# Second mixing after the dense step, norm's turning a step on, closer steps at the end: one schedule edit in a two-layer macaron network

## The chip, the cores and the metric

The kernel runs on one core of a Trainium2 chip. The metric is the device time of one execution in microseconds, the median of several runs. The profile is one execution, recorded by the hardware profiler. The engines are PE (TensorE), DVE (VectorE), ACT (ScalarE), POOL (GpSimd) and SP (SyncE, which issues DMAs).

## The reference, cut to what matters

2048 tokens (4 x 512) of width 128 pass through two macaron layers. Layer 0 is a routed expert network, a linear attention and the expert network again. Layer 1 is a product-key expert network, an attention of 16 heads whose scores are refined by a small network over all heads, and the product-key network again. The change lies in the last two of these, which the kernel computes joined.

```python
# attention of layer 1: the scores of all heads are mixed twice
attn_t = jnp.transpose(scores, (0, 2, 3, 1))
combined = jnp.concatenate([attn_t, kerple_t], axis=-1)
hdn = jax.nn.gelu(jnp.dot(combined, w1) + b1, approximate=False)
refined = jnp.dot(hdn, w2) + b2
scores = scores + kerple[None] + jnp.transpose(refined, (0, 3, 1, 2))
weights = jax.nn.softmax(jnp.where(causal, scores, -jnp.inf), axis=-1)
out = jnp.einsum('bhij,bhjd->bhid', weights, v)
# feed-forward of layer 1 behind it
q = (x @ Wq).reshape(b, t, 2, H, RET // 2)
sim = jnp.einsum('btphn,hkpn->pbthk', q, keys)
# top 8 of x keys, of y keys, of their 64 sums -> idx, scores
w = jax.nn.silu(jnp.einsum('btd,bthkd->bthk', x, down_embed[idx])) * jax.nn.softmax(scores)
x = x + 0.5 * (einsum('bthk,bthkd->btd', w, up_embed[idx]) + swiglu(x, Wg, bg, Wu, bu, Wd, bd))
```

## The kernel before, in words

`attn` (from line 976) holds the last two sublayers. It runs over 16 token tiles of 128 queries, four a batch. A tile with index `ib` in its batch sees `(ib + 1) * 128` keys. A **unit** (line 1176 on) is the part of a tile whose softmax is taken at once: the whole tile for `ib` 0 and 1, half a tile for 2 and 3. A unit is made of **pairs**: two for `ib` 0, four otherwise; 88 pairs in all. Names such as 11.1.6 say tile 11, half 1, row group 6.

A loop over **steps**, counted by `k` (lines 1341 to 1423), writes the order by hand. The four engines PE, DVE, ACT and POOL run strictly in that order (`manual_schedule`); one loop turn is a step, and nothing waits at its end: each engine goes on to the next step as soon as its own data are there. A step has, in this order:

- loads of the pair two steps on (SP; the pairs' score tiles F have ten buffers),
- `mix2` (line 1102) of the pair that was first mixed two steps before: 16 matmuls (L1107), then 2 to 8 reductions on DVE (L1118). If that pair was *busy*, its `mix2` comes only after the next two items,
- what is due by `at`: a unit's `norms` (L1194, L1196), `values` (L1217, L1229), `project` (L1234, L324), an expert tile's `norm` (L297) and `best` (L77, L78); then the turning of one pair of a finished unit (L1158, copied by L1164); then `middle`: the expert product (`turn`, `weigh`, `finish`: L184, L187, L199, L204) or the `gate` (L1289),
- either the **dense step** of an expert tile (L1272 on PE, then L1281 and L1283 on ACT), or `mix1` of the next pair: 32 matmuls (L1083) into a PSUM tile named `four`,
- `exps` of an expert tile if due (L118, L144, L153 with 4 exponentials), then the pair's GELU (L1098). A pair that comes right behind a unit's exponentials is *busy*: DVE copies it out of PSUM (L1094) and the GELU reads the copy,
- what is due by `end`: `near` (L84), `far` (L96), `tops` (L108, L111), `replace` (L118), `select` (L159), `heads` (L164, L166, L168), `last` (L174, L177), `turned` (L303, copied by L305), `add` (L324), and `finished`, which takes a tile's statistics (DVE L287, L288, then POOL L290, L291),
- if the step completed a unit, its exponentials (L1133: 16 for `ib` 0 and 1, 8 for the others), and, if an expert tile is ready, `norm8` (L133, L140) ahead of them. A step with both is called a **burst** here. `keys` of the next expert tile (L1262, L1264) come here too.

Two memories decide much. `four` takes half of PSUM and has one buffer, so `mix1` and the dense step follow one another through it: the next one starts when the GELU, the copy (L1094) or the gate has read the last one out. All small PSUM tiles are named `one` and go round four buffers: `mix2` takes two, a turning one or two, all others one.

A burst at step `k` sets the dense step to `k + 3`, the selection to `k + 4`, the expert product to `k + 7`. If a unit's softmax falls on the step ahead of the dense step, the dense step is put off by one. Written out, the loop takes 129 steps (0 to 128); the last `mix1` stands in step 100. Bursts stand in steps 19, 23, 31, 40, 44, 50, 57, 66, 70, 76, 83, 92, 96 and 102, dense steps among the mixings in 22, 26, 34, 43, 47, 54, 60, 69, 73, 80, 86, 95 and 99. ACT loads its function table anew whenever it goes from exponentials to GELU or to SiLU (dense) and back.

Of the kernel before, what the change touches and what calls it, by code (L numbers as in the profile page):

```python
# [211 lines left out]
class Net:  # L212
# [771 lines left out]
    def attn(self, out):  # L984

        nc, tc = self.nc, self.tc
        with (
# [11 lines left out]
            class Pair:  # L999
# [53 lines left out]
                def load(u):  # L1053

                    J, m = u.J, 2 * u.n
                    u.F = sf.tile([P, m, SEQ // u.n], FP, tag="F", name="F")
                    for half in range(2):
                        x = u.t.S[u.q0 + 4 * half : u.q0 + 4 * half + 4]
                        nc.sync.dma_start(
                            u.F[half::2, :, :J],  # L1060
                            bass.AP(
                                x.tensor, x.offset, [[SEQ, 4 * H], [-GQ * H * SEQ, m], [1, J]]
                            ),
                        )
# [239 lines left out]
            todo, middle, weights, late, stored = {}, {}, {}, {}, []  # L1304

            def at(k, f, *a):
                todo.setdefault(k, []).append((f, a))
# [4 lines left out]

            waiting, mixed, turns = list(pairs), {}, []
            ready, routed, last_u = [], None, None
            dense, turned, busy, k = -1, 0, False, 0

            def load(n):
                if n < len(pairs):
# [3 lines left out]
            def values_of(t):  # L1322
                v = s1.tile([P, H * DH], FP, tag="v", name="v", bufs=6)
                nc.sync.dma_start(v, t.v)
                vs[t.n] = v

            def finished(t):

                u = Experts(t.n)
                at(k + 1, u.norm)  # L1330
                end(k + 1, u.turned)
                end(k + 4, ready.append, u)

            def end(k, f, *a):
                late.setdefault(k, []).append((f, a))

            def run(todo):
                for f, a in todo.pop(k, ()):
                    f(*a)
# [4 lines left out]
            while len(stored) < NT:  # L1344
                if waiting and dense != k:
                    load(len(pairs) - len(waiting) + 2)
                second = mixed.pop(k - 2, None)
                if second and second is second.unit.parts[0] and not second.unit.q0:
                    values_of(second.t)
                if second and not second.busy:  # L1350
                    second.mix2()
                run(todo)
                if turns and turns[0][1] <= k:
                    p = turns.pop(0)[0]
                    p.turn()
                    if p is p.unit.parts[-1]:
                        n = max(k + 1, p.unit.end + 5)
                        at(n, p.unit.values)
                        if p.unit.q0 + p.unit.nq == P:
                            at(n + 1, project, p.t)  # L1360
                            end(n + 1, finished, p.t)
                run(middle)
                if second and second.busy:
                    second.mix2()
                first = None
                if dense == k:
                    last_u.dense()
                    middle.setdefault(k + 1, []).insert(0, (last_u.gate, ()))
                elif waiting:
                    first = waiting.pop(0)  # L1370
                    first.mix1(busy)
                    mixed[k], busy = first, False
                run(weights)
                if first:
                    first.gelu()
                    if waiting:
                        waiting[0].masks()
                run(late)

                full = second.unit if second and second is second.unit.parts[-1] else None  # L1380
                experts = fresh = None
                if routed and k >= routed.soonest and (full or not waiting and not mixed):
                    experts, routed = routed, None
                busy = busy or full is not None or experts is not None
                if not routed and ready:
                    routed = fresh = ready.pop(0)
                    fresh.soonest = k + 4
                    fresh.keys()
                if experts:
                    nc.scalar.preload_act_table_set("natural_log_exp_and_others")  # L1390
                    experts.norm8()
                if full:
                    full.softmax()
                    full.end = k + int(experts is not None)
                    late.setdefault(full.end + 2, []).insert(0, (full.invert, ()))
                    at(full.end + 3, full.norms)
                    if dense == k + 1 and waiting:
                        dense = k + 2
                    turns.extend((p, k + 2) for p in full.parts)
                if experts:  # L1400
                    u = last_u = experts
                    dense, turned = (k + 3 if waiting else max(k + 1, turned)), k + 7
                    weights[k + 1] = [(u.replace, (2, 3)), (u.shift, ()), (u.exps, ())]
                    end(k + 4, u.select)
                    end(k + 4, u.heads)
                    end(k + 6, u.last)
                    middle.setdefault(k + 7, []).extend(
                        (g, ()) for g in (u.turn, u.weigh, u.finish)
                    )
                    end(k + 7, u.add)  # L1410
                    at(k + 11, u.store)
                if fresh:
                    u = fresh
                    end(k + 1, u.near)
                    at(k + 2, u.best)
                    end(k + 2, u.far)
                    end(k + 3, u.tops, 0, 1, 2, 3)
                    end(k + 4, u.replace, 0, 1)
                k += 1
# [107 lines left out]
```

## Time and profile before

| what | value |
|---|---|
| median of 3 runs | 1616.69 us (1616.16 to 1617.67) |
| the profiled execution | 1613.29 us |
| its span, first to last instruction | 1611.5 us |
| PE busy | 1235.9 us (77%) |
| DVE busy | 933.4 us (58%) |
| ACT busy | 836.9 us (52%) |
| POOL busy | 828.2 us (51%) |
| first `mix1` (step 0) | 899.1 us |
| `mix1` of step 31, 57, 83, 96 | 1063.8, 1239.6, 1411.5, 1494.5 us |
| last `mix1` (step 100) | 1523.0 us |

How to read it: the times of the steps are the starts of the 32 matmuls of L1083 in that step, read off the timeline of PE, which runs them in the order of the loop. A row of the timeline has the start in us from the span's start, the time taken, engine, line, operation, what it writes and reads, the count of merged instructions, and in brackets the engine's idle time before it with what ended it. A row of the waits has the waiting engine and its tile, what it waited for, the sum in us, the number of waits and the longest.

### The profile page before, as it was taken

How to read it: one execution, taken by the hardware profiler on the slowest of the kernel's cores; microseconds unless marked ns; L12 is line 12 of the kernel's file. 1: busy time of each engine (PE TensorE's matmuls, PEld its weight loads, DVE VectorE, ACT ScalarE, POOL GpSimd, SP SyncE). 2: the span in 40 equal slices, each digit the busy share in tenths (PEclk: the TensorE clock that was granted, in tenths of full speed). 3: DMA queues.
4: the chain of work that ended last, by engine and by line, in shares of the span. 5: the costliest groups of instructions: out<-in, count | busy, mean ns of one | idle time of the engine just before them, and what ended most of it. 6: DMA issues, size and time to landing. Idle time of an engine off the chain costs nothing.

```text
span 1611.5 us, 32621 instructions
## 1 busy us (share of the span) xinstructions
PE 1235.9 (77%) x12520; PEld 800.2 (50%) x12520; DVE 933.4 (58%) x2540; ACT 836.9 (52%) x1653; POOL 828.2 (51%) x835
## 2 busy tenths in 40 slices
PE   5769989965888479888887588777778778777763
PEld 2446756643554255555663144554446445454462
DVE  6443422234543988787852267766757666766853
ACT  4211232211222657676654678855866666776752
POOL 4444232235443898888867046346544455436423
PEclk8889799977989689999998899889898889888986
DMA  4662032304220013444457977665555445545100
GB/s 101 153 165 54 0 68 59 73 15 106 53 54 0 0 53 137 159 145 166 156 199 261 289 212 208 200 178 155 138 162 180 129 148 149 168 127 151 30 11 4
DMA packets 182822, 194.08 MB, mean 120 GB/s; under 512 B 44058, under 2 KB 155018, under 8 KB 182538
## 3 DMA queue, kind: packets, MB, share of 16 engines
q1 hardware_dynamic: 181242, 190.87, 41.2%
q8 instruction: 99, 1.62, 0.4%
q10 hardware_dynamic: 1296, 1.11, 0.3%
q14 instruction: 57, 0.47, 0.1%
q0 software_dynamic: 128, 0.01, 0.0%
HBM read 139.96 MB, written 52.13 MB: 119 GB/s over the span
## 4 chain that ended last, share of the span: by engine, by line
PE 42%; DVE 17%; ACT 16%; POOL 14%; issue 7%; DMA 3%; SPq 1%; POOLq 0%; ACTq 0%; DVEq 0%
PE po L436 4%; ACT F L1133 4%; ACT ht L1098 4%; PE ph L1083 3%; PE pq L924 3%; PE pd L1272 3%; PE po L1217 3%; PE pf L1107 3%; POOL al L84 2%; PE pu L425 2%; ACT al L153 2%; PE pk L527 2%; PE pt L1158 2%; PE pg L423 2%; PE pu L549 2%
## 5 line engine op out<-in xcount | busy, mean ns | idle before, releaser
L1071 POOL TENSOR_TENSOR F<-F,kz 128x512 f32<-128x512 f32 (+10 forms) x88 | 164.3, 1869 | 78.3 <-ACT F L1133 61.1
L1118 DVE CUSTOM_DVE_ANT_0 F<-pf,F 128x64 f32<-128x64 f32 (+21 forms) x256 | 99.0, 435 | 143.4 <-PE pf L1107 121.6
L84 POOL TENSOR_TENSOR al<-sim 128x512 f32<-128x512 f32 x128 | 129.3, 1041 | 60.0 <-ACT sim L1264 51.5
L1098 ACT ACTIVATE ht<-ph,b 128x2048 f32<-128x2048 f32 (+7 forms) x65 | 102.1, 1571 | 107.8 <-PE ph L1083 107.7
L427 ACT ACTIVATE g<-pg 128x512 f32<-128x512 f32 x72 | 42.5, 597 | 184.8 <-PE pg L423 122.9
L1083 PE MATMUL ph<-rows,w1s 32*32 32x512 f32 (+16 forms) x2816 | 97.2, 580 | 50.8 <-issue 27.3
L1107 PE MATMUL pf<-ht,w2b 64*32 64x512 f32 (+16 forms) x1408 | 94.2, 561 | 47.3 <-ACT ht L1098 44.6
L1133 ACT ACTIVATE F<-F,mn 128x64 f32<-128x64 f32 (+21 forms) x256 | 129.5, 507 | 0.1
L164 POOL TENSOR_TENSOR al<-al 128x1152 f32<-128x1152 f32 x16 | 42.0, 2626 | 163.2 <-DVE al L159 130.7
L938 ACT ACTIVATE st<-pq 128x256 f32<-128x256 f32 (+3 forms) x128 | 82.8, 699 | 68.7 <-issue 37.9
L1158 PE MATMUL pt<-ident,F 128*128 128x128 f32 x640 | 102.8, 305 | 17.4 <-DVE mn L1118 7.6
L432 POOL TENSOR_TENSOR hT<-g,spread 128x512 f32<-128x512 f32 x64 | 79.6, 1266 | 65.3 <-DVE g L431 41.6
L1164 DVE COPY wT<-pt 128x512 f32<-128x512 f32 (+1 forms) x176 | 104.3, 632 | 11.9 <-PE pt L1158 10.0
L924 PE MATMUL pq<-k,q 32*128 32x256 f32 (+3 forms) x1024 | 101.7, 487 | 11.1 <-POOL q L901 8.2
L1158 PEld LDWEIGHTS pt<-ident,F 128*128 128x128 f32 x640 | 81.2, 157 | 50.1 <-ACT F L1133 18.8
L1217 PEld LDWEIGHTS po<-wT,v 128*64 128x64 f32 x2560 | 85.0, 150 | 24.6 <-issue 14.3
L118 DVE MATCH_REPLACE8 rep<-top,al 128x576 f32<-128x576 f32 x128 | 94.4, 741 | 0.0
L1217 PE MATMUL po<-wT,v 128*64 128x64 f32 x2560 | 88.6, 235 | 6.2 <-DVE wT L1164 4.8
L425 PE MATMUL pu<-ln_xT,w 128*128 128x512 f32 x144 | 80.3, 641 | 8.2 <-DVE g L431 4.8
L436 PEld LDWEIGHTS po<-w,hT 128*128 128x128 f32 x576 | 75.5, 213 | 8.4 <-POOL hT L432 5.4
L436 PE MATMUL po<-w,hT 128*128 128x128 f32 x576 | 77.2, 298 | 2.8 <-POOL hT L432 2.8
L894 DVE TENSOR_TENSOR t<-p,cos 128x512 f32<-128x512 f32 x64 | 43.8, 685 | 58.4 <-POOL k L902 34.2
(217 smaller groups left out, 2957.7 us busy)
## 6 DMA issues: line engine op xcount, KB each, us to landing
spread<-rows SPq DMA_DIRECT2D x24, 1024.0 KB
S<-st SPq DMA_DIRECT2D x32, 512.0 KB
S<-st SPq DMA_DIRECT2D x32, 384.0 KB
V<-v SPq DMA_DIRECT2D x16, 512.0 KB
S<-st SPq DMA_DIRECT2D x32, 256.0 KB
v<-V SPq DMA_DIRECT2D x16, 512.0 KB
rows<-near SPq DMA_DIRECT2D x12, 524.0 KB
F<-S SPq DMA_DIRECT2D x24, 256.0 KB
```

The costliest lines, as they stand in the source:

```text
L84: nc.gpsimd.tensor_tensor(u.al[:, h, :NEAR].rearrange("p (i j) -> p i j", j=NK), bc(u.sim[:, 0, h, :TK], 2, NK), bc(u.sim[:, 1, h], 1, TK) ...
L425: nc.tensor.matmul(pu, self.w3[:, c * P : (c + 1) * P], xT, start=True, stop=True)
L436: nc.tensor.matmul(po, hT[:, c, i * P : (i + 1) * P], self.w2[:, c, :], start=(c == 0), stop=(c == NCH),)
L924: nc.tensor.matmul(pq[hh // 2][:, hh % 2, :J], u.q[r, t, a, :], u.k[r, t, a, :J], start=(a == 0), stop=(a == 1), tile_position=(hh * 32, 0),)
L1071: nc.gpsimd.tensor_tensor(u.F[:, :, :J], u.F[:, :, :J], win, ALU.add)
L1083: nc.tensor.matmul(ph[32 * x : 32 * (x + 1), r, :, :J], self.w1s[at], u.G[x ^ 1][at], start=True, stop=True, tile_position=(32 * r, 32 * x),)
L1098: nc.scalar.activation(u.ht[:, :, :, : u.J], u.x, AF.Gelu, bias=self.b1)
L1107: nc.tensor.matmul(pf[c][32 * r : 32 * (r + 1), :, :J], self.w2b[at].rearrange("p h a -> p (h a)"), u.ht[at, r, :, :J], start=True, stop=True,
L1133: nc.scalar.activation(F, F, AF.Exp, bias=mn[:, g : g + 1], scale=-1.0, accum_out=sm[:, g : g + 1],)
L1158: nc.tensor.transpose(pt[:, at : at + P], u.F[:, m - 1 - s0 - s, j * P : (j + 1) * P], self.ident,)
L1164: nc.vector.tensor_copy(u.unit.wT[:, js.start : js.stop, :, q : q + w * GQ].rearrange("p j h (r q) -> p j h r q", q=2), pt[:, : len(js) * ...
L1217: nc.tensor.matmul(po[o * DH : (o + 1) * DH, c, :], vs[u.t.n - u.t.ib + j][:, h * DH : (h + 1) * DH], u.wT[:, j, h, x : x + nq], start=(j ...
```

## The change

Only the loop's bookkeeping changes; no instruction is added, dropped or resized.

- `mixed` now holds the step in which a pair's second mixing is due. It is two steps on as before, but three for the pairs first mixed in the two steps behind a burst, and never before the pair ahead of it. With the dense step at `k + 3`, those two second mixings come in the steps `k + 4` and `k + 5`, where before they came in `k + 3` and `k + 4`.
- `turned` comes two steps behind a tile's statistics, not one, while pairs are left. The tile is ready for its keys three steps behind, not four (one, once no pair is left).
- A tile may not start its burst until five steps behind its keys, not four, while pairs are left.
- The rule that put off a dense step behind a softmax is dropped.
- Once no pair is left, selection and heads come a step earlier behind the burst, last, product and add two steps earlier, and the next dense step may come two steps earlier.

```diff
-                end(k + 1, u.turned)
-                end(k + 4, ready.append, u)
+                end(k + 2 if waiting else k + 1, u.turned)
+                end(k + 3 if waiting else k + 1, ready.append, u)
...
-                second = mixed.pop(k - 2, None)
+                second = mixed.pop(k, None)
...
-                    mixed[k], busy = first, False
+
+                    due = max(due + 1, k + (3 if k in (burst + 1, burst + 2) else 2))
+                    mixed[due], busy = first, False
...
-                    fresh.soonest = k + 4
+                    fresh.soonest = k + (5 if waiting else 4)
...
-                    if dense == k + 1 and waiting:
-                        dense = k + 2
...
-                    u = last_u = experts
-                    dense, turned = (k + 3 if waiting else max(k + 1, turned)), k + 7
+                    u, burst = experts, k
+                    last_u = u
+                    dense, turned = (k + 3 if waiting else max(k + 1, turned)), k + (7 if waiting else 5)
...
-                    end(k + 4, u.select)
-                    end(k + 4, u.heads)
-                    end(k + 6, u.last)
-                    middle.setdefault(k + 7, []).extend(
+                    n = 0 if waiting else 1
+                    end(k + 4 - n, u.select)
+                    end(k + 4 - n, u.heads)
+                    end(k + 6 - 2 * n, u.last)
+                    middle.setdefault(k + 7 - 2 * n, []).extend(
...
-                    end(k + 7, u.add)
+                    end(k + 7 - 2 * n, u.add)
```

Written out, the loop now takes 126 steps, with the last `mix1` in step 99. Bursts stand in steps 19, 24, 31, 40, 45, 50, 57, 66, 71, 76, 83, 92, 97 and 102, dense steps among the mixings in 22, 27, 34, 43, 48, 53, 60, 69, 74, 79, 86 and 95, and dense step 12 in 100. Around the burst of step 57 (pairs 10.0.0 to 10.0.6), PE has:

| step | before | after |
|---|---|---|
| 58 | mix2, values 8, mix1 (busy), turned 7 | mix2, values 8, mix1 (busy) |
| 59 | mix2, project 8, turning, mix1 | mix2, project 8, turning, mix1, turned 7 |
| 60 | turning, mix2 (busy pair of 58), dense 6, turned 8 | turning, dense 6, keys 7 |
| 61 | mix2 (of 59), norms 9, turning, mix1, keys 7 | norms 9, turning, mix2 (busy pair of 58), mix1, turned 8 |
| 62 | turning, mix1 (busy) | mix2 (of 59), turning, mix1 |

On DVE the gate of step 61 stood behind the reductions of that step's mix2; now it stands ahead of them. From the end of the mixings on, PE's order was: dense 12, the last mix1, mix2, values 15.0, product 12, dense 13, keys 14, turnings, values 15.1, project 15, product 13, dense 14, turned 15, keys 15, product 14, dense 15, product 15. It is now: the last mix1, dense 12, mix2, mix2, turning, keys 14, values 15.0, turning, product 12, dense 13, turnings, product 13, dense 14, values 15.1, project 15, turned 15, keys 15, product 14, dense 15, product 15. On POOL, heads 14 stand ahead of the statistics of tile 15, where they stood behind them.

More of the change, by code (lines that the diff above doesn't have):

```diff
@@ L1314, in attn @@
             ready, routed, last_u = [], None, None
-            dense, turned, busy, k = -1, 0, False, 0
+            dense, turned, burst, due, busy, k = -1, 0, -9, 0, False, 0
             def load(n):
```

## The prediction

> **What bounds the kernel now.** I read the waits of the joined part first. It runs from 890 us to the end, and all of the change lies in it.
>
> ```profile
> engine line waited for: us in total, times, longest us
> PE pf L1107 <- ACT ht L1098: 44.6, 15, 6.2
> PE ph L1083 <- issue: 27.3, 13, 2.7
> PE pw L184 <- POOL ws L166: 23.0, 2, 16.5
> PE lt_pt L303 <- DVE lt_xn L297: 16.3, 8, 3.2
> ```
>
> These waits of TensorE are what the change touches: second mixings (L1107) behind a GELU, first mixings (L1083) after a dense step, the expert tail, norm's turning (L303). Are they on the path? I took dense step 60 in the timeline, ScalarE first, then TensorE, then VectorE.
>
> ```profile
> 1255.84 1.31 ACT L1098 ACTIVATE ht<-ht,b 128x1216 f32<-128x1216 f32 x1
> ...
> 1257.20 1.33 ACT L1098 ACTIVATE ht<-ph,b 128x1280 f32<-128x1280 f32 x1
> ```
> ```profile
> 1257.20 1.27 PE L1107 MATMUL pf<-ht,w2b 64*32 64x304 f32 x16 [6.20 <-ACT ht L1098]
> 1258.59 2.04 PE L1272 MATMUL pd<-lt_xT,downT 128*128 128x128 f32 x8
> 1260.45 1.06 PE L1272 MATMUL pd<-lt_xT,wg 128*128 128x128 f32 x8
> ...
> 1266.98 1.29 PE L1083 MATMUL ph<-rows,w1s 32*32 32x336 f32 x32 [2.02 <-issue]
> ```
> ```profile
> 1265.76 1.12 DVE L1289 SCALAR_TENSOR_TENSOR hT<-pd,bu,hT 128x128 f32<-128x128 f32 x4
> ```
>
> The two GELUs queue behind ScalarE's exponentials. The dense products (L1272) start 0.06 us after the second GELU ends (1258.53): they write the one PSUM tile that this GELU reads. In 11 of the 13 dense steps among the mixings this distance is 0.05 us. So the 6.2 us belong to ScalarE, and the second mixing in front of the dense step hides inside them. The 2.02 us put to "issue" end when the gate (L1289) lets that tile go, at 1266.88. From dense end to first mixing the 13 dense steps take 66.2 us, 4.4 to 6.7 each.
>
> **The change, part by part.**
>
> *Second mixings moved past the dense step.* Nothing is saved ahead of it: it still waits for the second GELU. Behind it, VectorE today does the second mixing's reduction (0.9 to 1.3 us), sT 0.27, wT 1.29, gate 1.12, so 5.1 us with the matmuls at dense step 73. After, the gate stands ahead of the reduction: pn 0.27, half the turning 0.5, wT 1.3, gate 1.1 make 3.2 to 3.4 us, with the moved mixing (1.1) beside it. Gain: 1.9 (step 22), 1.1 (34, a key matmul of 1.0 between), 1.1 (43), 1.7 (47), 0.3 (60, key matmul), 1.4 (69), 1.7 (73), 0.3 (86), 1.4 (95): 10.9 us offered.
>
> *A price that the waits view doesn't show.* Dense step 60's first eight matmuls took 2.04 us, the next eight 1.06. The Trainium skill ("TensorE: Matmul & The Clock Gate", Part 1) says that the array runs at half clock after an idle window, until about 3.4 us of activity. The row agrees: slow from 1257.20 to about 1260.5. Today the second mixing spends 1.3 us of that; after, the dense step spends all and takes about 4.9 us (step 86 took 4.88). From the rows 4.11, 4.59, 3.82, 4.15, 4.88, 4.77 that adds 0.8+0.3+1.1+0.7+0+0.1 = 3.0 us. By the plain count of matmuls it would be nothing. I take half, 1.5, as some of it falls where VectorE is last anyway.
>
> *Norm's turning one step on.* Of 16.3 us, those at steps 33 (3.2), 58 and 84 (1.3 each) lie in front of the same ScalarE wait: nothing. Those at 31 (1.3 of 2.2), 39, 65, 91 (2.8, 2.3, 2.3) and 15 (1.0) stand on the chain: 9.7 us offered. But the norm itself stays on VectorE in its step:
>
> ```profile
> 1288.59 2.15 DVE L297 TENSOR_SCALAR lt_xn<-x,lt_mv,lt_rs 128x128 f32<-128x128 f32 x1
> 1290.46 1.01 DVE L1164 COPY wT<-pt 128x512 f32<-128x512 f32 x2
> ```
>
> Behind it queue wT and the reduction, which free the four small PSUM tiles ("one") that the next second mixing needs. I worked step 60 to 66 through. Keys come a step earlier, so tops (0.9) and replace (1.5) now precede the statistics; norm runs 1288.9 to 1291.0, wT to 1292.0, reduction to 1293.0; turning and first mixing of step 66 start at 1293.0 and 1293.9 (before 1294.12); the exponentials at 1300.4 (before 1300.38). Gain nil. The norm took 0.33 us elsewhere and 2.15 with a mask running on GpSimd. The skill ("SBUF — State Buffer", Who interferes with whom) says that tensor_scalar can contend with GpSimd for a shared port pair, and the loser waits for a whole instruction. With 0.33 all of this would be 1.8 us sooner, 5.5 over three places; I keep the row's 2.15.
>
> *The rule that put the dense step off after a softmax is gone.* At 26, 54 and 80 the dense step now comes right behind 16 exponentials (5.75 us) and two table loads (1.28 each). I worked steps 66 to 83: first mixing at 70 is 1.5 sooner, one more GELU goes ahead of the exponentials, the dense step 74 starts at 1344.9 (its like, before, 1341.6, but with one mixing more done), the mixing of 12.0.0 at 1351.3 (before 1355.2), of 12.0.8 at 1355.9 (1362.4), the softmax of 12.0 ends at 1383.9 (1388.4). Then VectorE runs gate, reduction 1.0, GELU copy 2.0, invert 0.25, select 2.5, replace 1.5, reduction 1.1, sT 0.3, wT 1.3 in this order from 1387.2, so the last wT for values 11.1 is there at 1397.4 (before 1395.25). Values take 4.9; the mixing of 14.0.0 starts at 1404.3 (before 1404.16), that of 14.0.2 at 1412.2 (1411.46). The 4 to 6 us won are spent. Steps 31 to 57 repeat this: +0.7 each. Up to 31 the same way gives +1.1, less 0.6 for the turning at 15. Dense step 95's 1.4 stays. Main loop: 0.5+0.7+0.7-1.4 = +0.5, with the cold clock +2.0.
>
> *The end.* Let U be the first mixing of step 96 (1494.5); the span ends at U+117.0. After, the last two GELUs go ahead of dense step 12 (U+25), but the last softmax waits for VectorE: gate to U+31.6, reduction 1.3, select 2.5, replace 1.5, reduction 1.3, and key matmul, copy, table, norm8: U+41.7 (before U+36.7). Tile 13's select and heads then come when they came before (heads end U+63.0 against 63.2). Expert product 13 and dense 14 now precede values 15.1 on TensorE: values end at U+76.8 (before 68.2), tile 14's select at U+82.4 (81.4). Its heads on GpSimd now stand ahead of tile 15's statistics:
>
> ```profile
> 1568.83 0.22 POOL L290 TENSOR_SCALAR lt_rs<-lt_mv 128x1 f32<-128x1 f32 x1 [10.71 <-DVE lt_mv L288]
> ...
> 1576.04 2.61 POOL L164 TENSOR_TENSOR al<-al 128x1152 f32<-128x1152 f32 x1 [6.34 <-DVE al L159]
> ...
> 1580.49 4.04 POOL L84 TENSOR_TENSOR al<-sim 128x512 f32<-128x512 f32 x4
> ```
>
> Today L290 ran before the heads (L164). After: heads U+82.5 to 87.0, L290 and L291 to 87.8; VectorE's norm of tile 15 waits for them to U+88.2, with tile 14's last sum queued behind; TensorE's turning, key matmul and then product 14 (pw 1.1, po 1.9, 1.9) end at U+95.0 (before U+90.2), add 95.3, best 96.3, far 97.6, tops: norm8 of tile 15 starts at U+98.7, before 1588.53 or U+94.0. What follows it keeps its order (23.0 us). The end: +4.7, though the loop takes three steps less: what is left out, such as steps 112, 120 and 122, holds no instruction.
>
> *At nothing.* Table loads stay 1.28 each and in number but for one, inside the +4.7. Masks keep their place. SyncE: the F tiles are ten; twelve more loads (pairs of tiles 7, 11, 15) now wait for a turning just one step earlier, as those of steps 10 to 21 do today without TensorE waiting for one. A load has two steps to its mask, at 5 to 6 us a step against 3.2 us for F<-S in the chain. If that cover went, a mask would be some 3 us late in 12 steps.
>
> **Sum.** Main loop +2.0, end +4.7: +6.7. The profiled execution took 1613.29 us (span 1611.5), so 1620.0. The median of the runs shown is 1616.69, 3.4 more: 1623.4 us.
>
> **The rivals.**
>
> *Faster: the dense gap's gain lives.* One mechanism: the gate ahead of the reduction lets the first mixing start 0.3 to 1.9 us sooner at each dense step. If the steps behind are held by that mixing and not by VectorE's order, 10.9 and the turning's 9.7 stay, less 1.5 cold and plus 4.7 of the end: 1616.7-14.4 = 1602.3. For it: the gap is 66.2 us and every first mixing there waits for the gate; VectorE is busy 58% of the span. Against: in the two stretches that I worked through, VectorE's order took the gain back before the next burst. It decides the sign when more than 6.7 us of the 20.6 are kept.
>
> *No change: the end costs nothing.* If the compiler's placing of tiles lets the key matmul pass the last reductions (3 us), and heads 14 come 1.6 us sooner, the end is even and the main loop too: 1617. For it: most anchors I found move by under 1 us. Against: the order on GpSimd at the end is written down.
>
> *Slower by more.* The bursts lose another 7 us: dense steps quite cold (1.5 more), a norm of 2.15 us at three more places (3 times 1.8). 1623.4+7 = 1630. For it: such waits are what a walk by hand leaves out. Against: TensorE has idle time to hide them.
>
> That the change doesn't do what it says can be left out: the orders follow from the loop, and I wrote both out step by step.
>
> **The numbers.** Slower as summed 0.37, slower by more 0.20, faster 0.28, no change 0.15. About 0.2%, 3.2 us, is what a measurement of this kernel can tell from no change. So: faster 0.28, same 0.15, slower 0.57. The range goes from the faster rival, 1604, to beyond the slower one, 1633.
>
> **What would show it.** In the profile after: TensorE's wait for GELU moves from L1107 to L1272 (dense), some 35 to 45 us; the 27.3 us of "issue" at L1083 shrink to under 15; lt_pt waits for lt_xn under 3 us. From dense end to mixing about 3.3 us instead of 5.1. Dense steps behind a burst at 4.9 us. If the bursts then still start when they do today, the main loop is right; if they start steadily earlier, by 1 us or more a burst, it is wrong and the faster rival holds. At the end, L290 of tile 15 should run behind L164 of tile 14, and from the last GELU burst to the end some 5 us more; if the norm8 of tile 15 comes within U+94, the end is wrong.

## The result, and the profile after

The changed kernel takes 1638.5 us (median of 4 runs, 1635.85 to 1641.52) against 1617.07 us for the kernel before, run beside it: a ratio of 1.0134, 95% interval 1.0115 to 1.0152, so slower by 21.7 us (18.6 to 24.6). The prediction was 1623.4 us, with a range up to 1633: the direction held, the size did not. The profiled execution took 1638.07 us, with a span of 1636.1 us. Of its 24.6 us over the span of before, 2.5 are there at step 0 already, in code that the change does not touch.

Waits of TensorE after, in the joined part (columns as in the prediction):

```profile
engine line waited for: us in total, times, longest us
PE pd L1272 <- ACT ht L1098: 49.0, 13, 7.8
PE pt L1158 <- DVE mn L1118: 41.5, 21, 4.7
PE ph L1083 <- issue: 30.9, 13, 6.7
```

The wait for the GELU went from the second mixing to the dense products, as predicted (49.0 us, where 35 to 45 were foretold), and norm's turning (L303) waits for its norm no more. Two things are new. The turning of score tiles (L1158) waits 41.5 us for the second mixing's reductions on VectorE, where it waited 7.6 us. And the first mixing's wait at the dense steps, predicted at under 15 us, is 30.9; three dense steps, each right behind a softmax, have 6.67 us of it apiece. Dense step 60 in TensorE's timeline after:

```profile
1273.60 2.07 PE L1272 MATMUL pd<-lt_xT,downT 128*128 128x128 f32 x8 [7.79 <-ACT ht L1098]
1275.46 1.91 PE L1272 MATMUL pd<-lt_xT,wg 128*128 128x128 f32 x8
1277.17 1.92 PE L1272 MATMUL pd<-lt_xT,wu 128*128 128x128 f32 x8
...
1283.24 0.86 PE L1083 MATMUL ph<-rows,w1s 32*32 32x336 f32 x32 [0.94 <-issue]
```

The wait is 7.79 us with nothing in it; from the dense end (1279.09) to the first mixing it is 4.16 us instead of 4.57. This place is as predicted, only colder. The loss is elsewhere.

I cut the joined part at first mixings, which stand in the same order in every kernel, and sorted the stretches. *Long* are the three from the mixing of 3.1.2 to 6.0.2, 7.0.2 to 10.0.2, 11.0.2 to 14.0.2 (steps 19 to 31, 40 to 57, 66 to 83). *Short* are 6.0.2 to 7.0.2, 10.0.2 to 11.0.2, 14.0.2 to 15.0.2 (31 to 40, 57 to 66, 83 to 92). Then 92 to 96, and the *end* from step 96 on. Each row is one profiled execution, in us against before (317.6, 167.4, 28.4, 117.0). The stretch from step 0 to 19 is not in the table (+1.8 us in the changed kernel, -0.1 to +3.7 in the others).

A single stretch says less than the medians of the runs. e5 and the changed kernel have one order up to step 96 and still differ by 2 to 3 us in a stretch. e3, e7 and e11, which change the end alone, keep the order of before in all stretches but the last, and yet they take 4.2 to 4.9 us more in the first long one, most of it at dense step 26. There TensorE waited 2.7 to 3.0 us for a GELU and then ran with a granted clock of 0.50 (e3 and e11; 0.64 in e7), where before it had waited 0.75 us and kept 1.00. Before, then e11:

```profile
1026.82 1.09 PE L1107 MATMUL pf<-ht,w2b 64*32 64x512 f32 x16 [0.75 <-ACT ht L1098]
1028.04 1.16 PE L1272 MATMUL pd<-lt_xT,downT 128*128 128x128 f32 x8
```
```profile
1029.32 1.96 PE L1107 MATMUL pf<-ht,w2b 64*32 64x512 f32 x16 [3.00 <-ACT ht L1098]
1031.21 2.07 PE L1272 MATMUL pd<-lt_xT,downT 128*128 128x128 f32 x8
```

So the first number in the brackets below, against this one profile of before, is uncertain by some 4 to 5 us.

| kernel | long | short | 92 to 96 | end |
|---|---|---|---|---|
| changed | +16.0 (8.4, 5.3, 2.3) | +1.5 (-2.9, +2.9, +1.5) | -1.7 | +4.4 |
| e1 mixing and rule | +12.2 | -9.4 | -2.0 | +1.6 |
| e16 rule alone | +10.5 (0, 5.0, 5.5) | +0.1 | -0.2 | 0.0 |
| e2 turning alone | +1.7 | -6.0 | -0.7 | +1.5 |
| e6 mixing, rule, turning | +13.5 | -12.8 | -2.3 | -1.2 |
| e5 these and sooner keys | +21.7 | +1.2 | -2.5 | -1.4 |
| e15 changed, tops later at seven | +15.0 | -9.9 | -2.0 | +2.1 |
| e17 = e6, softmax behind dense | -3.3 | -13.6 | -2.1 | -1.0 |
| e18 both edits on the changed | -1.3 | -10.5 | -2.3 | +1.8 |

The predicted gain is there: e6 wins 12.8 us in the short stretches. In the changed kernel the sooner keys take it back, and the long stretches lose 16 us besides.

### The profile page after: what moved, and what is told of

Its sections match the earlier page's. It is cut to its first block, busy times and chain, and to the rows that moved or that the text cites. A ratio compares the mean times of both kernels' runs of the same rounds, so it can differ in the third digit from the quotient of the medians.

```text
span 1636.1 us, 32584 instructions
## 1 busy us (share of the span) xinstructions
PE 1234.5 (75%) x12520; PEld 802.5 (49%) x12520; DVE 937.9 (57%) x2540; ACT 834.3 (51%) x1650; POOL 829.4 (51%) x835
## 4 chain that ended last, share of the span: by engine, by line
PE 39%; DVE 21%; POOL 14%; ACT 12%; issue 6%; DMA 6%; SPq 1%; ACTq 0%; POOLq 0%; DVEq 0%
PE po L436 4%; ACT F L1133 4%; POOL al L84 3%; PE pd L1272 3%; PE pq L924 3%; PE po L1217 3%; PE ph L1083 3%; ACT ht L1098 3%; DVE rep L118 2%; PE pu L425 2%; DVE al L159 2%; PE pg L423 2%; PE pk L527 2%; PE pu L549 2%; PE po L204 2%
## 5 line engine op out<-in xcount | busy, mean ns | idle before, releaser
L164 POOL TENSOR_TENSOR al<-al 128x1152 f32<-128x1152 f32 x16 | 42.1, 2631 | 225.8 <-DVE al L159 225.8
L1158 PE MATMUL pt<-ident,F 128*128 128x128 f32 x640 | 96.0, 285 | 51.5 <-DVE mn L1118 41.5
L1118 DVE CUSTOM_DVE_ANT_0 F<-pf,F 128x64 f32<-128x64 f32 (+21 forms) x256 | 98.9, 435 | 59.6 <-PE pf L1107 55.2
L1083 PE MATMUL ph<-rows,w1s 32*32 32x512 f32 (+16 forms) x2816 | 94.6, 558 | 49.9 <-issue 30.9
L1158 PEld LDWEIGHTS pt<-ident,F 128*128 128x128 f32 x640 | 71.8, 144 | 86.0 <-issue 26.3
L1164 DVE COPY wT<-pt 128x512 f32<-128x512 f32 (+1 forms) x176 | 104.2, 632 | 11.2 <-PE pt L1158 10.5
L1217 PEld LDWEIGHTS po<-wT,v 128*64 128x64 f32 x2560 | 80.8, 144 | 18.7 <-issue 9.1
L1217 PE MATMUL po<-wT,v 128*64 128x64 f32 x2560 | 84.1, 229 | 0.0
L423 PE MATMUL pg<-ln_xT,w 128*128 128x512 f32 x144 | 78.9, 631 | 0.1
```

The costliest lines, as they stand in the source:

```text
L423: nc.tensor.matmul(pg, self.w1[:, c * P : (c + 1) * P], xT, start=True, stop=True)
L1083: nc.tensor.matmul(ph[32 * x : 32 * (x + 1), r, :, :J], self.w1s[at], u.G[x ^ 1][at], start=True, stop=True, tile_position=(32 * r, 32 * x),)
L1158: nc.tensor.transpose(pt[:, at : at + P], u.F[:, m - 1 - s0 - s, j * P : (j + 1) * P], self.ident,)
L1217: nc.tensor.matmul(po[o * DH : (o + 1) * DH, c, :], vs[u.t.n - u.t.ib + j][:, h * DH : (h + 1) * DH], u.wT[:, j, h, x : x + nq], start=(j ...
```

## The experiments

Times are ratios to the kernel before with their intervals; one thousandth is 1.6 us.

### The parts by themselves: e1 to e4

e1 adds to the kernel before:

```diff
-                second = mixed.pop(k - 2, None)
+                second = mixed.pop(k, None)
...
-                    mixed[k], busy = first, False
+                    due = max(due + 1, k + (3 if k in (burst + 1, burst + 2) else 2))
+                    mixed[due], busy = first, False
...
-                    if dense == k + 1 and waiting:
-                        dense = k + 2
```

> The kernel before with the mixing edit alone: second mixings three steps on behind a burst, and no putting off of the dense step behind a softmax (the two belong together). Theory (queue): the moved second mixings' reductions now stand on VectorE behind select and replace and keep the small PSUM tiles, so the turnings wait (L1158 for mn, 41.5 us after the whole change against 7.6 before): slower than before by 12 to 16 us, that wait over 25 us. Rival (keys): the loss comes from the earlier keys, whose tops then wait on VectorE for far on GpSimd: within 5 us of before here, that wait under 15 us. Rival (end): the loss is at the end: no slower than before here.

1.0007 (0.9992 to 1.0023): no difference. The L1158 wait is 27.5 us, and yet no time is lost in all: the theory that this wait is the price fell in its first form. The table says why: two effects cancel, a loss in the long stretches and a gain in the short ones.

e2:

```diff
-                end(k + 1, u.turned)
-                end(k + 4, ready.append, u)
+                end(k + 2 if waiting else k + 1, u.turned)
+                end(k + 4 if waiting else k + 1, ready.append, u)
```

> The kernel before with norm's turning alone a step on; the keys keep their step. Queue theory: harmless, 0 to 4 us faster, TensorE's wait of lt_pt for lt_xn from 16.3 us to under 3. Prediction on record: nil, since the norm itself still holds VectorE. Rival (keys): 0 to 4 us faster as well, since the keys stay.

0.9984 (0.9974 to 0.9995): 2.6 us faster. e2, e5 and e6 keep the change's sooner readiness of the last tiles (`k + 1`).

e3 is the end by itself:

```diff
-                    dense, turned = (k + 3 if waiting else max(k + 1, turned)), k + 7
+                    dense, turned = (k + 3 if waiting else max(k + 1, turned)), k + (7 if waiting else 5)
...
-                    end(k + 4, u.select)
-                    end(k + 4, u.heads)
-                    end(k + 6, u.last)
-                    middle.setdefault(k + 7, []).extend(
+                    n = 0 if waiting else 1
+                    end(k + 4 - n, u.select)
+                    end(k + 4 - n, u.heads)
+                    end(k + 6 - 2 * n, u.last)
+                    middle.setdefault(k + 7 - 2 * n, []).extend(
...
-                    end(k + 7, u.add)
+                    end(k + 7 - 2 * n, u.add)
```

> The kernel before with the closer steps at the end alone. The prediction's sum for the end gave +4.7 us, the two traces give +4.4 from step 96 on: slower by 3 to 5 us if the end's own order does it (statistics of tile 15 behind heads 14 on GpSimd). Rival: the end loses only because the last softmax comes later with the moved mixings: within 2 us of before.

1.0052 (1.0034 to 1.007): 8.4 us, more than expected. e4 is the changed kernel with turning and keys as before:

```diff
-                end(k + 2 if waiting else k + 1, u.turned)
-                end(k + 3 if waiting else k + 1, ready.append, u)
+                end(k + 1, u.turned)
+                end(k + 4, ready.append, u)
...
-                    fresh.soonest = k + (5 if waiting else 4)
+                    fresh.soonest = k + 4
```

> The whole change without the norm and key part (turning, readiness and the five steps to the burst as before). Queue theory: most of the 21 us stays, slower than before by 14 to 20 us. Rival (keys): 2 to 8 us slower than before, the end's share.

1.0052 (1.0038 to 1.0066): 8.4 us, as much as the end alone. So some 13 of the 21.7 us come in with the keys and the turning, though the turning alone gains.

### Keys or turning: e5 and e6

e5 is the changed kernel with the end as before (but for that readiness), e6 is e5 with the keys back as well, while pairs are left. From e5 to e6:

```diff
-                end(k + 3 if waiting else k + 1, ready.append, u)
+                end(k + 4 if waiting else k + 1, ready.append, u)
...
-                    fresh.soonest = k + (5 if waiting else 4)
+                    fresh.soonest = k + 4
```

> The changed kernel with only the end as before (select, heads, last and product of the last tiles at their old steps). Theory 'keys': with the second mixings due at k+3, keys, tops and replace that come a step sooner stand ahead of reductions on VectorE, and this costs 12 to 13 us in the main loop, the end about 8: so this kernel 12 to 14 us over before, TensorE's wait for mn at L1158 40 us or more. Rival 'sums': no part costs more than it did by itself (mixing +1.1, all but keys less end 0, turning -2.6), the rest comes only with the end: at most 3 us over before.

> As e5, but keys, tops and bursts at their old steps (a unit ready at k+4, soonest burst k+4); the turning stays a step later. Theory 'keys': without the sooner keys the loss is gone, -3 to +2 us against before, and L1158's wait for mn near that of the mixing alone (27 us in 18). Rival 'turning': the later turning itself, meeting late reductions on the four small PSUM tiles, makes the loss: 10 us or more over before here too.

e5 1.0108 (1.0081 to 1.0135), e6 0.9985 (0.9971 to 0.9998): 20 us apart, and all of it comes with the keys' step: the bursts stand in the same steps in both. The waits of TensorE, e6 and then e5:

```profile
PE pt L1158 <- DVE mn L1118: 29.6, 19, 5.2
```
```profile
PE pt L1158 <- DVE mn L1118: 40.5, 20, 4.7
```

Step by step the two traces part by jumps: 3.7 us at step 38, 2.3 at 64, 4.6 at 90, the rest in smaller ones. In the changed kernel it is the same at step 64 (GpSimd, VectorE, TensorE):

```profile
1297.40 0.64 POOL L96 TENSOR_TENSOR al<-sim,best 128x256 f32<-128x256 f32 x1
```
```profile
1298.07 0.87 DVE L108 MAX8 top<-al 128x8 f32<-128x128 f32 x4 [1.91 <-POOL al L96]
1298.98 0.85 DVE L111 TENSOR_SCALAR least<-top 128x4 f32<-128x4 f32 x1
1299.74 0.51 DVE L1118 CUSTOM_DVE_ANT_0 F<-pf,F 128x352 f32<-128x352 f32 x1
```
```profile
1296.60 0.60 PE L1158 MATMUL pt<-ident,F 128*128 128x128 f32 x4
1300.41 0.66 PE L1158 MATMUL pt<-ident,F 128*128 128x128 f32 x2 [3.21 <-DVE mn L1118]
```

With the keys a step sooner, the tops (L108) stand ahead of the second mixing's reduction (L1118). They wait 1.91 us for `far` on GpSimd, which stands behind `near` (4.05 us) and a mask. The reduction, ready long before, waits behind them; the small PSUM tile that it frees comes late, and TensorE's turning stops for 3.21 us in its middle. Tops and their wait thus cost TensorE 3 us, though TensorE uses nothing of theirs.

### Which of the sooner items: e8, e9, e10, e13, e14, e15

All but e15 start from e5. e8 puts the tops a step later for all tiles with pairs left, e9 the first two replaces too, e10 the tops of tiles 3, 7 and 11 only:

```diff
-                    end(k + 3, u.tops, 0, 1, 2, 3)
+                    end(k + (4 if waiting else 3), u.tops, 0, 1, 2, 3)
```
```diff
-                    end(k + 4, u.replace, 0, 1)
+                    end(k + (5 if waiting else 4), u.replace, 0, 1)
```
```diff
-                    end(k + 3, u.tops, 0, 1, 2, 3)
+                    end(k + (4 if waiting and u.i % 4 == 3 else 3), u.tops, 0, 1, 2, 3)
```

> e5 with the four tops a step later than the keys' order gives (k+4 for k+3, so where they stood before), and so behind the reductions of that step; keys and bursts stay sooner. Theory 'tops wait for far': tops7 waiting on VectorE for far7 on GpSimd holds the reductions that free the small PSUM tiles (3.2 us at step 64, and again 5 us at 28/54/80 where select and replace do it): with tops later 3 to 8 us less than e5. Rival: the loss at 28, 54 and 80 is by invert, select and replace, which do not move: less than 2 us changes.

> e5 with the tops and the first two replaces back at the steps they had before (tops at k+4, replace 0 and 1 at k+5 behind the keys, for all but the last tiles), so that of the sooner keys only the key products, their copy, the masks near and far on GpSimd and the best sums come a step sooner. Theory 'VectorE's tops and replace': the 16.5 us of e5 over e6 come from tops and replace standing ahead of the reductions that free the small PSUM tiles: then this is within 4 us of e6 (1614 to 1618). Rival 'GpSimd and the key products': near (4 us on GpSimd) and the key products a step sooner cost the time by themselves: 1625 us or more.

> e5 with the four tops a step later only for tiles 3, 7 and 11, whose tops stood ahead of the reduction and waited for far on GpSimd (TensorE's turning then waited 3 us and more; the steps 37, 63 and 89 lost 3.7, 2.3 and 4.6 us against e6). Theory 'tops wait for far': 10.6 us come back there, less 1.5 us each for tops and two replaces now in one step as in e8: 5 to 8 us less than e5's 1633.7, 1626 to 1629. Rival 'the slack is taken elsewhere': the next burst then waits for something else, and less than 2 us comes back.

e8 1.0207 (1.0183 to 1.0231), e9 1.0106 (1.009 to 1.0123), e10 1.007 (1.0048 to 1.0092). In e10 6 us come back. e8 and e9 were badly aimed. The three stalls did go (steps 38, 64, 90 were 3.6 to 4.6 us shorter in e8 than in e5), but the keys of tiles 1, 4, 5, 8, 9 and 12 are set off by the burst before them and come at the same step in e5 and e6. For these the edit made tops later than e6 has them, which lost 2.3 to 3.9 us around each of the steps 46, 51, 72 and 77 of e9. So e13 moves tops and replace only for the seven tiles whose keys do come sooner, e14 only for 3, 7 and 11, and e15 is the changed kernel whole with e13's edit:

```diff
-                    end(k + 3, u.tops, 0, 1, 2, 3)
+                    end(k + (4 if waiting and (not u.i or u.i % 4 > 1) else 3), u.tops, 0, 1, 2, 3)
-                    end(k + 4, u.replace, 0, 1)
+                    end(k + (5 if waiting and (not u.i or u.i % 4 > 1) else 4), u.replace, 0, 1)
```
```diff
+                    end(k + (4 if waiting and u.i % 4 == 3 else 3), u.tops, 0, 1, 2, 3)
+                    end(k + (5 if waiting and u.i % 4 == 3 else 4), u.replace, 0, 1)
```

> e5 with tops and the first two replaces back at their steps of e6, but only for the seven tiles whose keys come sooner at all (0, 2, 3, 6, 7, 10, 11): keys of 1, 4, 5, 8, 9, 12 are set by the burst before and come at the same step in e5 and e6, so that e8 and e9 put their tops later than e6 has them, and lost 2.3 to 3.9 us at each of the steps 46, 51, 72, 77. Key products, near, best and far stay sooner. Theory 'VectorE order': within 5 us of e6's 1613.7, so 1612 to 1619. Rival 'key products, near, far and best': nearly all of the 20 us stay, 1628 or more.

> As e13 for the tiles 3, 7 and 11 alone. Theory 'tops wait for far at these three': against e5's 1633.7 some 9 to 11 us come back (the steps 37, 63, 89 lost 3.7, 2.3, 4.6), 1622 to 1625, and the rest up to e13 belongs to tiles 0, 2, 6, 10. Rival 'all tiles alike': 3/7 of what e13 brings.

> The changed kernel whole, with the edit of e13. Theory: the main loop loses its 13 to 20 us and the end keeps its 4 to 9: 1619 to 1628 against 1638.5. Rival: the end took its part of the sooner keys' loss back already, and both sum to less: 1629 to 1635.

e13 1.0015 (1.0001 to 1.0028), e14 1.0023 (1.0012 to 1.0035), e15 1.0031 (1.002 to 1.0043). Tops and the first two replaces of three tiles, moved together, bring 13.7 us of e5's loss back (1.0108 to 1.0023), and in the changed kernel two edited lines bring 16.7 us back. e15 at step 64, VectorE and TensorE:

```profile
1289.87 0.53 DVE L1118 CUSTOM_DVE_ANT_0 F<-pf,F 128x352 f32<-128x352 f32 x1
...
1294.10 0.86 DVE L108 MAX8 top<-al 128x8 f32<-128x128 f32 x4
```
```profile
1290.31 0.82 PE L1158 MATMUL pt<-ident,F 128*128 128x128 f32 x6
```

Now the reduction goes first, the turning runs through without a stop, and the tops find `far` done. From e13 to e6 some 5 us remain (0.0030); they belong to the key products, `near`, `best` and `far`, or to the smaller jumps, and were not split further.

### Keys later still: e12

```diff
-                end(k + 4 if waiting else k + 1, ready.append, u)
+                end(k + 5 if waiting else k + 4, ready.append, u)
...
-                    fresh.soonest = k + 4
+                    fresh.soonest = k + (3 if waiting else 4)
```

> e6 (mixing, rule, turning; end as before) with the keys moved the other way: a unit ready at k+5 for k+4, and the soonest burst k+3 behind the keys for k+4, so that the bursts stay where they are. Theory 'tops and replace should stand behind the reductions': a step later they stand behind still more of them, but the burst's replace 2 and 3 come nearer to replace 0 and 1: 1608 to 1616, no worse than e6. Rival: the step of e6 is a best place, and a step later the exponentials wait for VectorE's tops and the least: 5 us or more over e6's 1613.7.

e12 starts from e6, and its last tiles are ready at `k + 4` again, as before the change. 0.9989 (0.9979 to 0.9999), no worse than e6 within the intervals. A step later costs nothing where a step sooner cost 20 us, which fits an order that is met or not, and no slope over the keys' step.

### The end: e7 and e11

e7 is e3 without its first hunk (the bound `turned` stays at `k + 7`), e11 moves select and heads only:

```diff
-                    end(k + 4, u.select)
-                    end(k + 4, u.heads)
+                    n = 0 if waiting else 1
+                    end(k + 4 - n, u.select)
+                    end(k + 4 - n, u.heads)
```

> Before with a part of the end's edit: select and heads a step, last and product two steps sooner for the last tiles, but the bound 'turned' (how soon the dense step of the next tile may come) at its old k+7. Whole end edit gave +8.4 in the profiled spans' ratio (1.0052). Theory 'POOL order': heads of a tile stand ahead of the next tile's statistics on GpSimd, and product ahead of values: all of it is in this part, so +7 to +10. Rival 'dense sooner': the loss comes from the dense step that the lower bound lets in ahead of the values, so here 0 to +2.

> Before with only select and heads of the last tiles a step sooner; last and product keep their old steps. e7 (product two steps sooner too) had +8.5 us. Theory 'product ahead of the keys': in e7 TensorE's product of tile 14 waits 10.3 us for GpSimd's heads, and the key product of tile 15, whose input has been turned, stands behind it (1592.3 against a turning at 1577.3): without the sooner product -1 to +3 us. Rival 'heads ahead of statistics or near': heads sooner on GpSimd hold near and best of the next tile (+2.6 us ahead of norm8 of 14): +4 to +9 here too.

e7 1.0062 (1.004 to 1.0084), e11 1.0019 (1.0008 to 1.003). e7 leaves the bound alone and costs no less than e3, so the bound is not what costs. TensorE in e7, then in e11:

```profile
1577.34 0.27 PE L303 MATMUL lt_pt<-ident,lt_xn 128*128 128x128 f32 x1
1587.95 1.11 PE L184 MATMUL pw<-ident,ws 128*128 128x128 f32 x4 [10.34 <-POOL ws L166]
...
1592.27 1.19 PE L1262 MATMUL psim<-wsim,lt_xT 128*128 128x512 f32 x2
```
```profile
1576.47 0.27 PE L303 MATMUL lt_pt<-ident,lt_xn 128*128 128x128 f32 x1
1578.50 1.12 PE L1262 MATMUL psim<-wsim,lt_xT 128*128 128x512 f32 x2 [1.76 <-ACT lt_xT L305]
```

In e7 the product of tile 14 (L184) waits 10.34 us for GpSimd's heads, and the keys of tile 15 (L1262), whose input was turned at 1577.6, stand behind it: the same kind of fault as with the tops. In e11 they go first. In the changed kernel they go first as well, because there a tile without pairs left is ready for its keys a step behind its statistics. That fits its end losing 4.4 us and not the 8 of e3, though no run took this apart. In e11 the norm8 of tile 14 still comes 2.8 us later than before. GpSimd before, then in e11:

```profile
1550.36 0.62 POOL L96 TENSOR_TENSOR al<-sim,best 128x256 f32<-128x256 f32 x1
1553.61 2.61 POOL L164 TENSOR_TENSOR al<-al 128x1152 f32<-128x1152 f32 x1 [2.63 <-DVE al L159]
```
```profile
1555.26 2.60 POOL L164 TENSOR_TENSOR al<-al 128x1152 f32<-128x1152 f32 x1
1560.29 0.62 POOL L96 TENSOR_TENSOR al<-sim,best 128x256 f32<-128x256 f32 x1
```

`far` of tile 14 (L96) ran ahead of heads 13 (L164 to L168, 4.5 us); now it stands behind them, and the tops of tile 14 wait 5.16 us for it on VectorE. `near` also took 6.35 us instead of 4.04 while the sooner selection ran on VectorE (3.27 us instead of 2.55). But the heads need that selection, which ended at 1554.4, so a shorter `near` would have let them begin at most 0.9 us sooner.

### The rule: e16, e17, e18

e16 only drops the rule:

```diff
-                    if dense == k + 1 and waiting:
-                        dense = k + 2
```

e17 is e6 with the softmax held back over a dense step, e18 the changed kernel with that and e13's edit:

```diff
+            held = None
...
+                if held:
+                    full, held = held, None
+                elif full and dense == k + 1 and waiting:
+                    full, held = None, full
```

> Before with one edit: the rule that puts a dense step off when a unit's softmax falls on the step ahead of it is gone (dense steps 1, 5, 9 come right behind 16 exponentials). In the profiles of e1, e6 and the changed kernel the stretches that hold them, steps 19 to 31, 40 to 57 and 66 to 83, are 6.6 to 8.4, 2.6 to 5.3 and 2.3 to 3.0 us longer than before, the others shorter. Theory 'dense behind the softmax': the rule alone makes this, 9 to 14 us over before. Rival 'order of the second mixings': the rule alone costs nothing, -3 to +3, and the second mixings in the third step make those stretches longer.

> e6 (second mixings in the third step, turning a step on, keys and end as before) with the softmax of such a unit held back by a step, so that it comes behind the dense step and not ahead of it; the dense step stays where it is. Theory 'dense behind the softmax': the 12 to 13 us of e6's three long stretches come back, less the step's delay of the unit's values: 1602 to 1609, faster than before and e6. Rival 'order of the second mixings', or the held softmax delays the values and the next burst as much: 1611 to 1618.

> The changed kernel whole, with the two edits that e15 and e17 make: tops and the first two replaces of the seven tiles a step later, and the softmax in front of a dense step held back behind it. Theory 'two causes': both add up, e15's 1.0031 less the 23 us that e17 gained on e6, so 1596 to 1603 against 1638.5, a few us over e17 for the end's sake. Rival: with the keys sooner the held softmax meets them on VectorE and most of the gain is lost: 1610 or more.

e16 1.0058 (1.0036 to 1.0081), e17 0.9843 (0.9819 to 0.9867), e18 0.9889 (0.9862 to 0.9916). Dense step 53 in the changed kernel, TensorE and ScalarE:

```profile
1219.88 1.06 PE L1272 MATMUL pd<-lt_xT,wu 128*128 128x128 f32 x8
...
1229.30 1.06 PE L1083 MATMUL ph<-rows,w1s 32*32 32x448 f32 x16 [6.67 <-issue]
```
```profile
1217.96 1.28 ACT L1133 ACT_TABLE_LOAD   x1
...
1225.11 1.28 ACT L1281 ACT_TABLE_LOAD   x1
1226.40 0.60 ACT L1281 ACTIVATE sP<-pd 128x512 f32<-128x512 f32 x1
```

The dense products are done at 1220.94, but ScalarE reads them out from 1226.40 on, behind a table load and 16 exponentials, and only then do the gate and the first mixing follow: 8.36 us from dense end to mixing, at steps 27, 53 and 79 alike. In the kernel before, these three dense steps (26, 54 and 80) have 5.80, 5.33 and 6.67 us; at 80, which comes a step behind its softmax:

```profile
1388.66 1.06 PE L1272 MATMUL pd<-lt_xT,wu 128*128 128x128 f32 x8
...
1396.39 2.02 PE L1083 MATMUL ph<-rows,w1s 32*32 32x512 f32 x32 [0.53 <-issue]
```

e17 at its dense step 53:

```profile
1206.97 1.06 PE L1272 MATMUL pd<-lt_xT,wu 128*128 128x128 f32 x8
...
1211.04 1.05 PE L1083 MATMUL ph<-rows,w1s 32*32 32x448 f32 x32 [1.32 <-issue]
```

From dense end to mixing it is 3.01 us. e17 takes 1592.07 us (1590.84 to 1597.01): by the ratios 23 us less than e6, and faster than both kernels by far. In its profile, which is the slowest of its four runs, the long stretches go from e6's +13.5 to -3.3. That is more than the 12 to 13 us that were to come back: the held softmax is a new order and not the old rule, and part of what it brings can be a gain of its own. e18 takes 1601.31 us, where the changed kernel took 1638.5. With both orders mended, nothing of the main loop's loss is left.

## Why the prediction was wrong in size

- *Nothing saved ahead of the dense step, the gate ahead of the reduction*: right. All 12 dense steps start 0.05 us behind the second GELU. At the nine that are not behind a softmax, dense end to mixing is 2.93 to 4.16 us (3.2 to 4.4 predicted, with a key matmul or without). These and the turning do win: 12.8 us in e6's short stretches and 2.3 behind them, of 20.6 offered. The rival "the gap's gain lives" was right on these parts, and the statement "gain nil" was wrong for them.
- *The cold clock*: right in kind. The six dense steps behind a burst that the prediction priced went from 26.3 to 28.8 us, +2.5 where 3.0 was the full and 1.5 the taken price; step 22, not priced, added 2.4.
- *The rule dropped*: **this step failed.** The prediction walked one stretch, 66 to 83, to +0.7 us, wrote "Steps 31 to 57 repeat this: +0.7 each", and gave +0.5 up to 31: 1.9 us in sum, where the long stretches have +16.0 in the changed kernel and +13.5 in e6. The walked stretch was not far off: it took +2.3. Reckoned from the mixing of 11.0.2, its gate comes 0.5 us sooner than walked and its last wT 1.5 us later, and one term of that is VectorE's copy (L1094), which waits 1.10 us for the first mixing. The two siblings did not repeat it: they took +5.3 and +8.4. e16 gives the rule's own price, about 5 us a place: 5.0 and 5.5 at the two dense steps (54 and 80) where it acts in the kernel before. The moved mixings give 2.4 us of it back at each (e1 has 2.6 and 3.1). At 26 it acts only once the mixing edit has moved that burst from step 23 to 24, so e16 has 0.0 there and e1 6.6; how much of this first stretch is the rule, how much the colder dense step 22 and how much the scatter shown above is not known. "The 4 to 6 us won are spent" is where the sum went wrong: more than these is spent. Behind dense step 79 the gap from dense end to mixing is 8.35 us, and then the turning of step 81 stops for the reductions of step 80, which VectorE takes up only behind a copy, a selection of 2.50 us and two replaces:

```profile
1410.13 2.50 DVE L159 SCALAR_TENSOR_TENSOR al<-rep,al 128x2304 f32<-128x2304 f32 x1
```
```profile
1415.18 1.09 PE L1158 MATMUL pt<-ident,F 128*128 128x128 f32 x4 [4.07 <-DVE mn L1118]
```

- *Keys a step sooner* (in the prediction under norm's turning): **this step failed as well, and it is the larger.** "Tops (0.9) and replace (1.5) now precede the statistics ... Gain nil": the tops were priced by their busy time. They also wait 1.9 us for `far`, and what they delay is not only the statistics but the reduction ahead of those, and by its PSUM tile TensorE. From dense step 60 to the mixing of step 66 the prediction had 35.3 us, as before (35.5); it took 38.7. In sum over the short stretches this hid the 12.8 us that the other parts won, and so the stretches came out at +1.5, close to the predicted nil for the wrong reason.
- *The end*: right. +4.4 us against +4.7, with statistics of tile 15 (L290) behind heads 14, as GpSimd shows after, and norm8 of tile 15 at U+98.4 (predicted U+98.7):

```profile
1597.26 2.61 POOL L164 TENSOR_TENSOR al<-al 128x1152 f32<-128x1152 f32 x1 [16.76 <-DVE al L159]
...
1601.73 0.22 POOL L290 TENSOR_SCALAR lt_rs<-lt_mv 128x1 f32<-128x1 f32 x1
```

The sum by the ratios: mixing, rule and turning -2.4 us (e6); sooner keys +19.9 (e5 less e6), of which tops and replace of tiles 3, 7, 11 make 13.7 (e5 less e14); the end +4.2 (changed less e5). Together +21.7. The rival "slower by more" put 7 us more on the bursts for cold dense steps and norms; the direction was right and the cause another.

What stays open: sooner keys without the moved mixings were not tried, nor the moved mixings with the rule kept, so whether each costs the same there is not known. The held softmax was not tried on the kernel before, so how much of its 23 us is a gain of its own is open. Nor is the residue of some 5 us between e13 and e6 traced to one cause.

## What to carry to other kernels

On an engine that runs in order, price a moved instruction by what it can wait for and by who stands behind it, not by its busy time; look first for the instruction behind it that frees a buffer of another engine. When one PSUM tile passes between two uses, put the instruction that reads it out ahead of any long block, even if that block is ready first. A stretch walked by hand says nothing of its siblings until the same instructions are seen beside each other there; and a part that shows no difference when tried alone may hide a loss and a gain of one size.

## What was not expected of the hardware

Dense step 60 ran all its 24 matmuls at half clock: 2.07, 1.91 and 1.92 us for eight each, with a granted clock of 0.50 from 1273.6 to 1279.1. Steps 22 and 95 did nearly the same (5.37 and 5.48 us). Steps 34 and 43 had the full clock in the third group (2.08, 1.74, 1.06 us at 34). The idle wait does not tell them apart: it is 7.79 us ahead of 60 and of 34 alike, and 3.78 ahead of 22. Shorter waits were enough as well: 3.00 us in e11 (0.50 from 1029.3 to 1034.7), and in e7 the whole of dense step 22 was slow (5.49 us, 0.50 from 1002.9 to 1008.3) behind waits of 1.86 and 0.79 us with a second mixing between them. The Trainium skill ("TensorE: Matmul & The Clock Gate", Part 1) gives about 3.4 us of activity until the clock is full: steps 34 and 43 agree, 22, 60 and 95 took over 5 us, and the measurement decides. Tops' last instruction (L111, 128x4) took 0.36 us in e6 at step 38 and 0.84 us in e5 at step 37 while a mask ran on GpSimd, as the norm's 0.33 and 2.15 us do; its cost is in what waits behind it.
